# Two attention-convolution layers on one core: bands in four transfers, shorter table slots, x turned from lanes of seven rows, fold one column later

## The chip, the cores and the metric

The kernel runs on one core of a Trainium2 chip, in float32. The metric is the device time of one execution in microseconds (us), the median of several runs. A profile is one further execution, recorded instruction by instruction and DMA packet by DMA packet.

## What is computed

```python
x = x + layer0(group_norm(x))      # x: 8 x 56 x 56 x 384
x = x + layer1(group_norm(x))

def layer0(x):                     # 12 heads of 32 channels, window of 3 x 3
    v = x @ Wv.T                   # every pixel: a value of 384 channels
    a = x @ Wa.T                   # every pixel: 12 heads x 9 x 9 logits
    attn = softmax(a * 32 ** -0.5, axis=-1)
    out = attn @ patches_3x3(v)    # 9 outputs per pixel, from its 9 neighbours
    y = sum of the 9 outputs, each added at the pixel that it belongs to
    return y @ Wo.T

def layer1(x):                     # 6 heads of 64 channels, window of 3 x 3
    a = softmax(x @ W_attn + b)    # every pixel: 6 heads x 9 weights
    v = x @ W_v + b_v
    y = sum over the 9 neighbours of a * v
    return y @ W_proj + b_proj
```

In layer 0, attention of 9 x 9 followed by the addition comes to one linear map from a 5 x 5 neighbourhood of `v` to each pixel, with weights of its own for each pixel and head.

## The kernel before, in words

**Pairs and columns.** The eight images are taken two at a time: four pairs, in each of which a column is 2 x 56 = 112 rows (`R`). Layer 0 goes through the 4 x 56 columns in one loop (line 1007), a step for each column and `LAG` = 3 steps behind it. All seven columns of eight fill 128 partitions: the eighth column's rows are shared out among the 16 spare partitions of the other seven (`OVER`, `share_out`). Its own step has no attention.

**A step.** `attend` (line 685) projects the column to logits in three parts (`bank<-wa_t`), and to values (`bank<-wv_t`). VectorE subtracts the maximum, ScalarE takes the exponential. One step later `normalise` (line 758) sums on VectorE (`d`, `den`) and multiplies on GpSimd (`at<-at,den`). Two steps later `presum` (line 771) adds on GpSimd what the three columns give to one column's weights (`pre`, 9 x 5 x 12 a row); two of its five slices are copied by ScalarE. Three steps later `fold` (line 806) adds over neighbouring rows: ScalarE writes scaled slices to a weight slot of `wts`, TensorE moves rows by a product with `shift` (`pw<-pre,shift`), VectorE adds. SyncE then writes the slot to a table in HBM (`ztab<-wts`). There are four slots in `wts` (`NWT`), so a new column's slices wait until an older slot has been written.

**Bands.** The output is made by patches of 7 x 7 pixels. For a strip of seven columns (`px`) and one image, the table `ztab0` is read back as a matrix `z` (line 383, `bands`): a partition for each of 11 x 11 source pixels of a patch, and for each of eight patches, seven output rows of 12 heads x 7 columns. The table's lines are skewed by one row for each image row, so that one access pattern picks the right weights. A source pixel touches only five output rows, in places that shift with its row; the other entries are zeros of the table. The kernel before reads all seven rows for all 128 partitions in one transfer (`GROUPS0`), and for this a table slot has 11 rows (`EP0`): three of zeros, five of weights, three of zeros. Layer 1 has a table of its own kind, read as two transfers of 45 partitions (`GROUPS1`). `vp<-vtab` reads the values in the same form. `pc<-z,vp` multiplies both, `po<-yT,wo_t` is the last projection.

**Turning x.** [...] x comes with pixels on rows. For pair 0 TensorE turns it. For pairs 1 to 3 this is done while the pair before is worked on, from column 3 to column 45: a block of four columns each three steps. `stats_load` (line 483) brings a block in four transfers, one for each 96 channels: 28 partitions each, on a partition four rows ("lanes") by four columns by 96 channels. VectorE transposes blocks of 32 x 32 (line 524), and gets 128 places for 112 rows, 16 of them empty; `keep_block` (line 550) writes the 112 to HBM (`xT<-xt`) in 12 pieces a partition. ScalarE sums x and its square for the norm.

**What sets the order.** TensorE and GpSimd run in program order, and after line 1002 ScalarE and VectorE too. Each engine's list follows from the loop: `between(0)` to `between(3)` put the work of older columns behind the parts of the projection. Strips are read by `fetch_v` and `fetch_z` at fixed distances behind the loop (line 1062), counted from `LAG`; contractions and output projections are jobs with due steps after that (`plan`, line 874). SyncE issues nearly all DMAs, in its own program order. After its last column layer 0 runs `LAG` steps without attention; then layer 1 starts, while jobs of layer 0's last strips still run.

Of the kernel before, what the change touches and what calls it, by code (L numbers as in the profile page):

```python
# [8 lines left out]
F32 = mybir.dt.float32  # L9
# [6 lines left out]
def two_outlook_layers(  # L16
# [34 lines left out]
    B, H, W, C = x.shape  # L51
    P = 128
    NCH = C // P
    IMG = 2
    R = IMG * H
    MARGIN = 2
# [6 lines left out]
    XB = 4  # L63
# [6 lines left out]
    HEADS0, HEADS1 = 12, 6  # L70
    D0, D1 = C // HEADS0, C // HEADS1
    K, K2 = 3, 9
    E0 = 2 * K - 1
# [4 lines left out]
    PH = K * HEADS0  # L78
# [5 lines left out]
    PY1, NPY1, SX1, SY1 = 8, 7, PX + 2, 10  # L84
    ROW1 = HEADS1 * PX

    GROUPS0 = (((0, P), (0, 7)),)
    GROUPS1 = (((0, 45), (0, 5)), ((45, 90), (3, 8)))

    EP0, FIRST0 = 11, 3
    EP1, FIRST1 = 11, 4
    SLOT0, SLOT1 = EP0 * ROW0, EP1 * ROW1
    LINE0, LINE1 = SX0 * SLOT0 + ROW0, SX1 * SLOT1 + ROW1
# [4 lines left out]
    QC = NCH * Q  # L101
    NR = 4
    LANES = R // NR

    def by_quadrant(ap, r0, col, n, b):
        first = r0 * W * C + col * C + b * QC
        return bass.AP(ap.tensor, ap.offset + first, [[W * C, R], [C, n], [1, QC]])
# [94 lines left out]
        outside(0, 0, R + b * PART)  # L202
        outside(NTILE - 1, 2, R + b * PART + PART - 1)

    NZERO = (EP0 - E0) * ROW0
    zeros = const.tile([R, NZERO], F32, name="zeros")
    gpsimd.memset(zeros, 0.0)

    def fill(table, first, dims, width):

        src = zeros[: dims[0][1], :width]
        if len(dims) > 1:
            src = src.unsqueeze(1).to_broadcast([dims[0][1], dims[1][1], width])
        tc.keep_in_program_order(
            nc.sync.dma_start(bass.AP(table.tensor, table.offset + first, [*dims, [1, width]]), src)
        )
# [22 lines left out]
    def clear_first():  # L239

        clear_v(vtab0, SX0, 2)
        fill(ztab0[0], MARGIN * LINE0 + FIRST0 * ROW0, [[LINE0, R], [SLOT0, 2]], E0 * ROW0)
        clear_weights(ztab0[0], LINE0, 366, SX0, SLOT0, ROW0, FIRST0, E0, EP0)

    def clears():

        yield 3, lambda: clear_weights(
            ztab0[1], LINE0, 366, SX0, SLOT0, ROW0, FIRST0, E0, EP0
        )
        yield (NPAIR - 1) * W + 4, lambda: clear_v(vtab1, SX1, 1)  # L250
        for n, t in enumerate(ztab1):
            yield (NPAIR - 1) * W + 10 + 8 * n, lambda t=t: clear_weights(
                t, LINE1, 350, SX1, SLOT1, ROW1, FIRST1, K, EP1
            )
# [214 lines left out]
    def layer0(late, pools):  # L469
# [6 lines left out]
        stats, st1s, params, xins, attns, pres, xrs, xts = {}, {}, {}, {}, {}, {}, {}, {}  # L476

        def block_tile(pair, blk):
            t = io.tile([P, XB * NCH * P], F32, tag="xt", name=f"xt_{pair}_{blk}")
            n = P if pair else R  # L480
            return t[:, : XB * NCH * n].rearrange("p (m i r) -> p m i r", m=XB, i=NCH)

        def stats_load(pair, blk, queue, xr):
            xrs[pair, blk] = xr
            if not pair:
                queue.dma_start(xr, xf[:R, blk * XB : (blk + 1) * XB, :])
                return
            for b in range(NQ):
                queue.dma_start(
                    xr[b * Q : b * Q + LANES].rearrange("p s m c -> p (s m c)"),  # L490
                    by_quadrant(x, pair * R, blk * XB, XB, b),
                )

        xr_bufs = [io.tile([P, XB * C], F32, tag=f"xr{n}", name=f"xr_{n}", bufs=1) for n in range(2)]
        for t in xr_bufs:
            vector.memset(t[P - Q :], 0.0)

        def xr_tile(pair, blk):
            t = xr_bufs[blk % 2]
            if not pair:  # L500
                return t[:R].rearrange("r (m c) -> r m c", m=XB)
            return t.rearrange("p (s m c) -> p s m c", s=NR, m=XB)

        NWT = 4
        wts = fixed.tile([P, NWT, E0 * HEADS0 * PX], F32, name="wts0")
# [2 lines left out]
        def stats_chunk(pair, blk, i):  # L508

            if blk == 0 and i == 0:  # L510
                if pair:
                    stats[pair] = Sums(f"0_{pair}", NBLK)
                else:
                    stats[pair] = stat.tile([P, IMG, NCH, NBLK, 6], F32, tag="st0", name=f"st0_{pair}", bufs=1)
            if i == 0 and pair:
                xts[pair, blk] = block_tile(pair, blk)
            xr, xt = xrs[pair, blk], xts[pair, blk]
            if pair == 0:
                pt = bank(P, 0, XB * R).rearrange("p (m r) -> p m r", m=XB)
                for j in range(XB):  # L520
                    transpose(pt[:, j, :], xr[:, j, i::NCH], ident[:R, :R])
                scalar.copy(xt[:, :, i, :], pt)
            else:
                vector.transpose(
                    xt[:, :, i, :].rearrange("p m (k s) -> p s m k", s=NR), xr[:, :, :, i::NCH]
                )
            yield
            if pair == 0:
                for b in range(IMG):
                    vector.bn_stats(stats[pair][:, b, i, blk, :], xt[:, :, i, b * H : (b + 1) * H])  # L530
            if i == NCH - 1:
                del xrs[pair, blk]
                if pair:
                    keep_block(pair, blk)
                    if blk == 0:
                        stats[pair].start(lambda b, i: xt[:, :, i, b * H : (b + 1) * H])
                    summed.append((stats[pair], blk, xt.rearrange("p m i r -> p i m r")))
            yield
# [11 lines left out]
        def keep_block(pair, blk):  # L550

            tc.keep_in_program_order(
                nc.sync.dma_start(
                    xTs[pair][:, blk * XB : (blk + 1) * XB].rearrange("p m i r -> p (m i) r"),
                    xts.pop((pair, blk)).rearrange("p m i r -> p (m i) r")[:, :, :R],
                )
            )

# [199 lines left out]
        def normalise(pair, c):  # L758

            nm, at = f"0_{pair}_{c}", attns[pair, c]  # L760
            d4 = work.tile([P, K, 4, PH], F32, tag="d4", name=f"d4_{nm}", bufs=1)
            vector.tensor_add(d4, at[:, :, 0:4], at[:, :, 4:8])
            vector.tensor_add(d4[:, :, 0:2], d4[:, :, 0:2], d4[:, :, 2:4])
            vector.tensor_add(d4[:, :, 0], d4[:, :, 0], d4[:, :, 1])
            den = work.tile([P, K, PH], F32, tag="den", name=f"den_{nm}", bufs=1)
            vector.tensor_add(den, d4[:, :, 0], at[:, :, 8])
            vector.reciprocal(den, den)
            vector.tensor_mul(den, den, inside[:, c % SB].unsqueeze(2).to_broadcast([P, K, PH]))
            gpsimd.tensor_tensor(at, at, den.unsqueeze(2).to_broadcast([P, K, K2, PH]), ALU.mult)

        def presum(pair, c):


            pre = work.tile([R, K2, E0, HEADS0], F32, tag="pre", name=f"pre_{pair}_{c}")

            def of(t, f, n):

                a = attns.get((pair, c + t))
                if a is None:
                    return None  # L780
                a = a[:R].rearrange("r pi (qi qj) (pj h) -> r (pi qi) qj pj h", qj=K, pj=K)
                return a[:, :, 1 - t, f - 1 - t : f - 1 - t + n, :]

            def put(f, n, *terms):
                dst, terms = pre[:, :, f : f + n, :], [t for t in terms if t is not None]
                if len(terms) == 1:
                    gpsimd.tensor_copy(dst, terms[0])
                else:
                    gpsimd.tensor_tensor(dst, terms[0], terms[1], ALU.add)

            put(1, 2, of(0, 1, 2), of(-1, 1, 2))
            yield
            put(3, 1, of(0, 3, 1), of(1, 3, 1))
            put(2, 1, pre[:, :, 2:3, :], of(1, 2, 1)) if c + 1 < W else None
            pres[pair, c] = pre
            yield
            for f, t in ((0, -1), (4, 1)):
                term = of(t, f, 1)
                if term is None:
                    gpsimd.memset(pre[:, :, f : f + 1, :], 0.0)  # L800
                else:
                    scalar.copy(pre[:, :, f : f + 1, :], term)
            attns.pop((pair, c - 1), None)
            yield

# [158 lines left out]
        def upkeep(step):  # L964

            pair, c = divmod(step, W)
            if pair == 0:
                if c == 1:
                    gpsimd.memset(wts, 0.0)
                if c == 3:  # L970
                    by = z_flat[0][:, : NCH * C].rearrange("p (i n) -> p i n", i=NCH)
                    sync.dma_start(by, wo0.rearrange("(i p) n -> p i n", p=P))
                if 5 <= c < 5 + NCH:
                    by = z_flat[0][:, : NCH * C].rearrange("p (i n) -> p i n", i=NCH)
                    sort_columns(wo_t, by, c - 5, vector.tensor_copy)
# [27 lines left out]
        xins.update({blk: homes[blk] for blk in range(4)})  # L1003
        normed(0, WHOLE, both=True)
        normed(1, SHARED, both=True)
        LAG = 3
        for step in range(NPAIR * W + LAG):
            folding = fold(*divmod(step - LAG, W)) if step >= LAG else iter(())
            turning = turned(step)
# [401 lines left out]
```

## Time and profile before

| | us |
|---|---|
| median of three timed runs | 3240.69 (3239.91 to 3242.24) |
| profiled execution, its own time | 3246.89 |
| its span, first to last instruction | 3245.2 |
| PE busy / DVE / ACT / POOL | 3043.9 / 2015.7 / 1386.3 / 1551.5 |

PE is TensorE, DVE VectorE, ACT ScalarE, POOL GpSimd, SP SyncE. Layer 0 takes the first two thirds of the span; its pairs begin at 68, 582, 1108 and 1629 us. The page's row of DMA load has 16 engines; "share" is the part of their time that packets took. A wait in an answer on waits reads: who waited for whom, us in total, times, longest.

The trace also holds every packet. Those of SyncE's queue can be told apart by their size:

| transfer | packet | direction | partitions of SBUF | packets, 582 to 1108 us | mean ns | median ns |
|---|---|---|---|---|---|---|
| `z<-ztab` | 2352 B | in | 128 | 16384 | 107.0 | 95 |
| `vp<-vtab` | 1536 B | in | 128 | 16325 | 72.3 | 65 |
| `xin<-xT` | 5376 B | in | 128 | 1792 | 279.9 | 206 |
| `xr<-in_x` | 384 B | in | 28 | 25088 | 33.3 | 22 |
| `xT<-xt` | 448 B | out | 128 | 21504 | 28.6 | 26 |
| `ztab<-wts` | 1008 B | out | 112 | 9408 | 53.2 | 46 |

Elsewhere: `ztab<-zeros` (2016 B, out of 112 partitions) 96.0 and 82 between 68 and 320 us; in layer 1 between 2250 and 3200 us `z<-ztab` (840 B into 45 partitions) 69.6 and 65, of which the fastest twentieth takes 40; `vp<-vtab` (1536 B into 90 partitions) 104.6 and 104; `out<-ot` (384 B, out of 28 partitions) 23.7 and 22.

### The profile page before, as it was taken

How to read it: one execution, taken by the hardware profiler on the slowest of the kernel's cores; microseconds unless marked ns; L12 is line 12 of the kernel's file. 1: busy time of each engine (PE TensorE's matmuls, PEld its weight loads, DVE VectorE, ACT ScalarE, POOL GpSimd, SP SyncE). 2: the span in 40 equal slices, each digit the busy share in tenths (PEclk: the TensorE clock that was granted, in tenths of full speed). 3: DMA queues.
4: the chain of work that ended last, by engine and by line, in shares of the span. 5: the costliest groups of instructions: out<-in, count | busy, mean ns of one | idle time of the engine just before them, and what ended most of it. 6: DMA issues, size and time to landing. Idle time of an engine off the chain costs nothing. (4 is left out here: it accounts for less than half of the span.)

```text
span 3245.2 us, 72428 instructions
## 1 busy us (share of the span) xinstructions
PE 3043.9 (94%) x27136; PEld 2041.3 (63%) x27136; DVE 2015.7 (62%) x4519; ACT 1386.3 (43%) x3584; POOL 1551.5 (48%) x2319
## 2 busy tenths in 40 slices
PE   6789999998999999998999999979999999999998
PEld 5556666666666766666666677645655656655655
DVE  5767766767776677776666666614545554545454
ACT  4345554555555455555454454433221312222221
POOL 2654554554455555555555555544343334343431
PEclk8899999999999999999999999989999999999998
DMA  9799997899999899999788897788889889989997
GB/s 287 210 280 293 302 290 255 274 294 285 281 274 308 255 276 297 288 300 287 252 274 274 286 303 247 254 309 219 227 229 234 240 231 238 239 233 233 240 232 160
DMA packets 745409, 850.83 MB, mean 262 GB/s; under 512 B 406286, under 2 KB 632210, under 8 KB 736738
## 3 DMA queue, kind: packets, MB, share of 16 engines
q1 hardware_dynamic: 647890, 711.32, 75.4%
q0 software_dynamic: 63824, 116.90, 11.6%
q10 hardware_dynamic: 33344, 17.98, 2.1%
q8 instruction: 214, 3.51, 0.5%
q14 instruction: 137, 1.12, 0.1%
HBM read 514.86 MB, written 322.17 MB: 258 GB/s over the span
## 5 line engine op out<-in xcount | busy, mean ns | idle before, releaser
L128 PE MATMUL bank<-wa_t,xn 128*128 128x288 f32 x3528 | 978.9, 415 | 4.0 <-ACT xn L143 4.0
L128 PE MATMUL po<-yT,wo_t 128*128 128x448 f32 (+1 forms) x2304 | 826.0, 501 | 43.1 <-ACT yT L143 23.5
L143 POOL TENSOR_TENSOR at<-at,den 128x972 f32<-128x972 f32 x196 | 442.4, 2257 | 801.2 <-DVE den L143 441.3
L128 PEld LDWEIGHTS bank<-wa_t,xn 128*128 128x128 f32 x3528 | 658.2, 193 | 216.6 <-issue 19.0
L128 PEld LDWEIGHTS po<-yT,wo_t 128*128 128x128 f32 x2304 | 439.6, 192 | 361.3 <-issue 199.6
L143 ACT COPY yT<-pc 128x294 f32<-128x294 f32 (+2 forms) x512 | 192.4, 401 | 727.4 <-PE pc L128 727.0
L1185 POOL DMA_DIRECT2D at<-lgt x392 | 204.8, 526 | 595.0 <-DVE lgt L143 585.0
L128 PE MATMUL bank<-wc_t,xn 128*128 128x438 f32 x1176 | 477.1, 542 | 1.3 <-DMA wc_t<-in_wv 1.3
L143 DVE TENSOR_REDUCE mx<-bank 128x36 f32<-128x324 f32 x588 | 279.4, 475 | 314.7 <-PE bank L128 312.9
L128 PEld LDWEIGHTS pc<-z,vp 121*32 121x32 f32 (+1 forms) x17664 | 340.6, 121 | 149.8 <-issue 99.9
L128 PE MATMUL pc<-z,vp 121*32 121x49 f32 (+1 forms) x17664 | 377.4, 219 | 44.9 <-issue 19.1
L143 ACT ACTIVATE at<-at 128x972 f32<-128x972 f32 (+1 forms) x228 | 215.2, 944 | 475.2 <-DVE at L143 474.2
L128 PE MATMUL bank<-wv_t,xn 128*128 128x384 f32 x1176 | 416.5, 491 | 0.0
L128 PEld LDWEIGHTS bank<-wc_t,xn 128*128 128x128 f32 x1176 | 215.0, 190 | 176.2 <-issue 163.1
L143 POOL TENSOR_TENSOR pre<-at,at 112x108 f32<-112x108 f32 (+1 forms) x440 | 239.4, 544 | 166.7 <-DMA at<-last 80.7
L128 PEld LDWEIGHTS bank<-wv_t,xn 128*128 128x128 f32 x1176 | 222.8, 191 | 132.7 <-issue 10.2
L143 DVE TENSOR_TENSOR at<-bank,mx 128x324 f32<-128x324 f32 x588 | 291.3, 495 | 20.3
L143 POOL DMA_DIRECT2D vtab<-v x476 | 289.4, 612 | 16.2 <-DMA vtab<-zeros 6.8
L143 ACT ACTIVATE unused<-x1t,shift 128x672 f32<-128x672 f32 (+1 forms) x256 | 200.7, 784 | 178.1 <-DVE x1t L143 152.9
L143 ACT ACTIVATE wts<-pre,inside 112x48 f32<-112x48 f32 (+4 forms) x672 | 179.7, 355 | 207.6 <-DMA ztab<-wts 189.4
L143 DVE TENSOR_TENSOR lgt<-bank,ba_t 128x54 f32<-128x54 f32 x196 | 42.1, 215 | 308.2 <-PE bank L128 303.5
L372 POOL DMA_DIRECT2D vtab<-v x392 | 211.6, 544 | 14.2 <-issue 7.0
(120 smaller groups left out, 2847.3 us busy)
## 6 DMA issues: line engine op xcount, KB each, us to landing
z<-ztab SPq DMA_DIRECT2D x64, 2352.0 KB
vp<-vtab SPq DMA_DIRECT2D x64, 1536.0 KB
vp<-vtab SPq DMA_DIRECT2D x64, 945.0 KB
xres<-xT SPq DMA_DIRECT2D x32, 1176.0 KB
ztab<-wts SPq DMA_DIRECT2D x336, 110.2 KB
vtab<-v POOLq DMA_DIRECT2D x108, 336.0 KB, 6.8
xin<-xT SPq DMA_DIRECT2D x52, 672.0 KB
z<-ztab SPq DMA_DIRECT2D x128, 258.4 KB
```

The lines of the kernel that those rows point to most:

```text
L128: tc.keep_in_program_order(nc.tensor.matmul(*args, **kwargs))
L143: return lambda *args, **kwargs: tc.keep_in_program_order(op(*args, **kwargs))
L372: queue.dma_start(bass.AP(table.tensor, table.offset + first, [*([line * step, count] for step, count in rows_of or ((1, rows),)), *([[(R ...
L1185: nc.gpsimd.dma_start(at_of(g_of)[row : row + n, m_of].rearrange("r k h -> r (k h)"), lg[lo : lo + n])
```

## The change

- `GROUPS0`: a band is read in four transfers of 32 partitions, with the three or six rows that can differ from zero there. The rest of `z` is set to zero once, in six pieces on GpSimd in columns 8 to 13.
- `EP0`: a table slot has 8 rows instead of 11; lines and zero fills get shorter.
- x is loaded so that a partition holds seven rows of two columns: eight transfers of 16 partitions a block instead of four of 28, as many packets of 384 B. Two transposes of 7 x 32 take the place of one of 16 x 32, and give 112 places without gaps, so that `xT<-xt` is one piece of 5376 B a partition.
- `LAG` goes from 3 to 4; the fold and all reads and jobs behind it move by a step. `pre` has three buffers instead of two, and `den` is a part of `d4` that is free by then.
- The two copies of `presum` go from ScalarE to GpSimd.

```diff
@@ -84,13 +84,13 @@
     PY1, NPY1, SX1, SY1 = 8, 7, PX + 2, 10
     ROW1 = HEADS1 * PX
 
-    GROUPS0 = (((0, P), (0, 7)),)
+    GROUPS0 = (((0, 32), (0, 3)), ((32, 64), (0, 6)), ((64, 96), (1, 7)), ((96, P), (4, 7)))
     GROUPS1 = (((0, 45), (0, 5)), ((45, 90), (3, 8)))
 
 
 
 
-    EP0, FIRST0 = 11, 3
+    EP0, FIRST0 = 8, 3
     EP1, FIRST1 = 11, 4
     SLOT0, SLOT1 = EP0 * ROW0, EP1 * ROW1
     LINE0, LINE1 = SX0 * SLOT0 + ROW0, SX1 * SLOT1 + ROW1
@@ -101,6 +101,7 @@
     QC = NCH * Q
     NR = 4
     LANES = R // NR
+    NS = 2 * R // Q
 
     def by_quadrant(ap, r0, col, n, b):
         first = r0 * W * C + col * C + b * QC
@@ -202,7 +203,7 @@
         outside(0, 0, R + b * PART)
         outside(NTILE - 1, 2, R + b * PART + PART - 1)
 
-    NZERO = (EP0 - E0) * ROW0
+    NZERO = C
     zeros = const.tile([R, NZERO], F32, name="zeros")
     gpsimd.memset(zeros, 0.0)
 
@@ -239,13 +240,15 @@
     def clear_first():
 
         clear_v(vtab0, SX0, 2)
-        fill(ztab0[0], MARGIN * LINE0 + FIRST0 * ROW0, [[LINE0, R], [SLOT0, 2]], E0 * ROW0)
-        clear_weights(ztab0[0], LINE0, 366, SX0, SLOT0, ROW0, FIRST0, E0, EP0)
+        for n in range(2):
+            first = MARGIN * LINE0 + FIRST0 * ROW0 + n * SLOT0
+            fill(ztab0[0], first, [[LINE0, R], [E0 * ROW0 // 2, 2]], E0 * ROW0 // 2)
+        clear_weights(ztab0[0], LINE0, 267, SX0, SLOT0, ROW0, FIRST0, E0, EP0)
 
     def clears():
 
         yield 3, lambda: clear_weights(
-            ztab0[1], LINE0, 366, SX0, SLOT0, ROW0, FIRST0, E0, EP0
+            ztab0[1], LINE0, 267, SX0, SLOT0, ROW0, FIRST0, E0, EP0
         )
         yield (NPAIR - 1) * W + 4, lambda: clear_v(vtab1, SX1, 1)
         for n, t in enumerate(ztab1):
@@ -476,9 +479,8 @@
         stats, st1s, params, xins, attns, pres, xrs, xts = {}, {}, {}, {}, {}, {}, {}, {}
 
         def block_tile(pair, blk):
-            t = io.tile([P, XB * NCH * P], F32, tag="xt", name=f"xt_{pair}_{blk}")
-            n = P if pair else R
-            return t[:, : XB * NCH * n].rearrange("p (m i r) -> p m i r", m=XB, i=NCH)
+            t = io.tile([P, XB * NCH * R], F32, tag="xt", name=f"xt_{pair}_{blk}")
+            return t.rearrange("p (m i r) -> p m i r", m=XB, i=NCH)
 
         def stats_load(pair, blk, queue, xr):
             xrs[pair, blk] = xr
@@ -486,20 +488,20 @@
                 queue.dma_start(xr, xf[:R, blk * XB : (blk + 1) * XB, :])
                 return
             for b in range(NQ):
-                queue.dma_start(
-                    xr[b * Q : b * Q + LANES].rearrange("p s m c -> p (s m c)"),
-                    by_quadrant(x, pair * R, blk * XB, XB, b),
-                )
+                for n in range(2):
+                    lo = b * Q + n * Q // 2
+                    queue.dma_start(
+                        xr[lo : lo + Q // 2].rearrange("p s m c -> p (s m c)"),
+                        by_quadrant(x, pair * R, blk * XB + n * XB // 2, XB // 2, b),
+                    )
 
         xr_bufs = [io.tile([P, XB * C], F32, tag=f"xr{n}", name=f"xr_{n}", bufs=1) for n in range(2)]
-        for t in xr_bufs:
-            vector.memset(t[P - Q :], 0.0)
 
         def xr_tile(pair, blk):
             t = xr_bufs[blk % 2]
             if not pair:
                 return t[:R].rearrange("r (m c) -> r m c", m=XB)
-            return t.rearrange("p (s m c) -> p s m c", s=NR, m=XB)
+            return t[:, : XB // 2 * NS * QC].rearrange("p (s m c) -> p s m c", s=NS, c=QC)
 
         NWT = 4
         wts = fixed.tile([P, NWT, E0 * HEADS0 * PX], F32, name="wts0")
@@ -521,9 +523,11 @@
                     transpose(pt[:, j, :], xr[:, j, i::NCH], ident[:R, :R])
                 scalar.copy(xt[:, :, i, :], pt)
             else:
-                vector.transpose(
-                    xt[:, :, i, :].rearrange("p m (k s) -> p s m k", s=NR), xr[:, :, :, i::NCH]
-                )
+                for n in range(XB // 2):
+                    vector.transpose(
+                        xt[:, n :: XB // 2, i, :].rearrange("p m (k s) -> p s m k", s=NS),
+                        xr[:, :, n, i::NCH],
+                    )
             yield
             if pair == 0:
                 for b in range(IMG):
@@ -551,8 +555,8 @@
 
             tc.keep_in_program_order(
                 nc.sync.dma_start(
-                    xTs[pair][:, blk * XB : (blk + 1) * XB].rearrange("p m i r -> p (m i) r"),
-                    xts.pop((pair, blk)).rearrange("p m i r -> p (m i) r")[:, :, :R],
+                    xTs[pair][:, blk * XB : (blk + 1) * XB].rearrange("p m i r -> p (m i r)"),
+                    xts.pop((pair, blk)).rearrange("p m i r -> p (m i r)"),
                 )
             )
 
@@ -762,7 +766,7 @@
             vector.tensor_add(d4, at[:, :, 0:4], at[:, :, 4:8])
             vector.tensor_add(d4[:, :, 0:2], d4[:, :, 0:2], d4[:, :, 2:4])
             vector.tensor_add(d4[:, :, 0], d4[:, :, 0], d4[:, :, 1])
-            den = work.tile([P, K, PH], F32, tag="den", name=f"den_{nm}", bufs=1)
+            den = d4[:, :, 1]
             vector.tensor_add(den, d4[:, :, 0], at[:, :, 8])
             vector.reciprocal(den, den)
             vector.tensor_mul(den, den, inside[:, c % SB].unsqueeze(2).to_broadcast([P, K, PH]))
@@ -771,7 +775,7 @@
         def presum(pair, c):
 
 
-            pre = work.tile([R, K2, E0, HEADS0], F32, tag="pre", name=f"pre_{pair}_{c}")
+            pre = work.tile([R, K2, E0, HEADS0], F32, tag="pre", name=f"pre_{pair}_{c}", bufs=3)
 
             def of(t, f, n):
 
@@ -799,7 +803,7 @@
                 if term is None:
                     gpsimd.memset(pre[:, :, f : f + 1, :], 0.0)
                 else:
-                    scalar.copy(pre[:, :, f : f + 1, :], term)
+                    gpsimd.tensor_copy(pre[:, :, f : f + 1, :], term)
             attns.pop((pair, c - 1), None)
             yield
 
@@ -970,6 +974,9 @@
                 if c == 3:
                     by = z_flat[0][:, : NCH * C].rearrange("p (i n) -> p i n", i=NCH)
                     sync.dma_start(by, wo0.rearrange("(i p) n -> p i n", p=P))
+                if 8 <= c < 14:
+                    b, n = divmod(c - 8, 3)
+                    gpsimd.memset(zs[b][:, 3 * n : min(NPY0, 3 * n + 3)], 0.0)
                 if 5 <= c < 5 + NCH:
                     by = z_flat[0][:, : NCH * C].rearrange("p (i n) -> p i n", i=NCH)
                     sort_columns(wo_t, by, c - 5, vector.tensor_copy)
@@ -1003,7 +1010,7 @@
         xins.update({blk: homes[blk] for blk in range(4)})
         normed(0, WHOLE, both=True)
         normed(1, SHARED, both=True)
-        LAG = 3
+        LAG = 4
         for step in range(NPAIR * W + LAG):
             folding = fold(*divmod(step - LAG, W)) if step >= LAG else iter(())
             turning = turned(step)
```

## The prediction

> **What bounds the kernel now.** The profiled execution took 3246.89 us (span 3245.2, 1.7 around it), 6.2 above the median of the three timed runs, 3240.69. I read the stretches first, cut where layer 0 changes its load: pair 1 with the turning of pair 2's x (600 to 1010), its end without turning (1010 to 1108), the same for pair 2, then pair 3, which turns nothing (1629 to 2029). Columns are the stretch, its length, the busy time of PE, PEld, DVE, ACT and POOL, the granted clock, DMA share and GB/s.
>
> ```profile
> 600.00:1010.00 410.00, 382.15 (x3802) 268.07 (x3801) 293.60 (x688) 227.40 (x573) 214.44 (x284) 0.98 0.95 288
> 1010.00:1108.00 98.00, 92.39 (x715) 63.84 (x714) 63.71 (x168) 52.87 (x133) 52.96 (x71) 0.98 0.77 248
> 1126.00:1530.00 404.00, 379.66 (x3799) 266.52 (x3798) 293.93 (x689) 227.71 (x573) 214.17 (x282) 0.98 0.98 292
> 1629.00:2029.00 400.00, 390.65 (x4057) 277.54 (x4056) 266.31 (x674) 194.72 (x499) 224.27 (x297) 1.00 0.84 277
> ```
>
> With turning, the DMA engines are at 0.95 to 0.98 and PE has gaps; without it DMA falls to 0.84, PE fills and more matmuls go through (4057 in 400 us against 3802 in 410). The first matmul of column 46 comes 443.0, 438.1 and 409.1 us after that of column 0 in pairs 1, 2 and 3 by the rows of `wv_t`. So three times some 30 us hang on DMA load, in the turning stretches. Layer 1 has PE at 99 to 100% in nearly every 100 us; little changes there.
>
> Next, who waits, in pair 1 (582 to 1108), in three answers: ACT's waits, PE's, and SyncE's own.
>
> ```profile
> ACT at L143 <- DVE at L143: 94.7, 40, 7.6
> ACT wts L143 <- DMA ztab<-wts: 59.6, 17, 9.2
> ```
>
> ```profile
> PE po L128 <- ACT yT L143: 7.0, 2, 3.8
> PE pw L128 <- issue: 6.8, 5, 2.8
> PE pw L128 <- POOL pre L143: 5.4, 3, 1.8
> PE pw L128 <- ACT pre L143: 4.7, 1, 4.7
> ```
>
> ACT stands 59.6 us until a weight slot has been written out; in pair 3 that wait is 8.5. [...] ACT's later work (`yT`, `pre`) queues behind the wait. DMA is what has to be costed.
>
> **Costs on the DMA engines, per pair.** The table ahead gives packet times; a sum over 16 engines is count x mean / 16. Pair 1 keeps them busy 0.923 x 526 = 486 us.
>
> (a) *Bands.* Now 16 x 1024 = 16384 packets of 2352 B: 16384 x 107 / 16000 = 109.6 us. After: 8192 of 1008 B and 8192 of 2016 B, bytes down from 2352 to 1512 KB a band. Packets of these sizes exist: median 46 ns (`ztab<-wts`) and 82 ns (`ztab<-zeros`), both out of SBUF. If bands ran like that, with the 12% that 2352 B has over its own 95: 8192 x (52 + 92) / 16000 = 74, a gain of 36. But every load into fewer than 128 partitions is slow in this trace: layer 1's bands (45 partitions, 840 B) take 69.6 at a fastest of 40, 1.74 times; its `vp` (90 partitions) takes 104.6 where layer 0's equal packets into 128 take 72.3. By 1.74: 8192 x (80 + 143) / 16000 = 114, a loss of 5. [...] The nearest row is 45 wide, the change 32, so I go between: **+12** (-36 to +21).
>
> (b) *x loads.* Per block four transfers of 28 partitions become eight of 16, still 1792 packets of 384 B. Now 25088 x 33.3 / 16000 = 52.2 us. [...] From the trace: 1536 and 2352 B into 128 partitions differ by 30 ns for 816 B, 27 B/ns[...]. By the row they replace alone, nothing changes. [...] **+30** (0 to +41).
>
> (c) *Turned x written out.* 21504 packets of 448 B, 28.6 ns, 38.4 us, become 1792 of 5376 B; `xin<-xT`, the same size inward, takes 206 at the median and 280 in the mean: 23 to 31. **-11** (-15 to -7).
>
> Sum +31 a pair: 517 for 486. The turning stretch holds three quarters of the bands and all of the rest, +28. Its engines already run near full; the heaviest 100 us slices show 0.99. Pair 1: (0.95 x 410 + 28) / 0.99 = 422, +12. Pair 2: (0.98 x 404 + 28) / 0.99 = 428, +24. Pair 0 between 200 and 488 (0.96 of 288, some 19 of the 28): 299, +11. **+47.** Pair 3 gets its bands' +12 at a share of 0.84: nothing.
>
> **The rest.**
> - *LAG 4 at the start.* Up to 320 us PE waits for `pw` 7.7 + 4.0 and 9.4 + 5.5 + 5.1 us, the fold being right behind the presum. A column between takes part of it, but DVE and POOL set the pace there (DVE 103 of 132 us from 68 to 200). With the first table's zero fill (1232 packets of 2016 B at 96 ns to 1008 B at 54, 3.2 us, at 92 to 118 us): **-8** (-15 to 0).
> - *LAG 4 elsewhere.* In the turning stretches the `pw` waits give way to the next DMA wait. In the three stretches without turning (DMA 0.77) **-3** (-12 to 0).
> - *LAG 4 at the end.* One more step without attention. The last `pw` groups start 3 to 5 us apart (2113.90, 2117.18, 2121.92, 2126.16): **+4** (0 to +8).
> - *Copies to POOL.* 440 x 282 ns leave ACT (26 a pair), 440 x 276 (POOL's four like copies) join POOL, 30 a pair, at the column's end. Queued behind are the next column's `pre` and `at` multiply. POOL waits 105.7 us a pair for DVE's `den`, which covers them; uncovered, +30 a pair. What ACT gains is lost in its DMA wait: 0.
> - *Transposes.* 126 of 512 elements at 1132 ns become 252 of 224. The `ot` transposes (512: 1107, 384: 887) give 1.72 ns an element over 227, so 612 each: +92 ns x 42, 4 us a pair on DVE, which waits 74 us a pair for PE; 4 if uncovered. `den` inside `d` makes the next column's first add wait for POOL's multiply; at 2096.96 that had ended 1.5 us before. 0 to 4 in all.
> - *z memsets.* Four of 1764 and two of 1176 elements at 0.86 ns (4704 take 4038): 8 us on POOL in columns 8 to 13 of pair 0, POOL half idle: 0.
> - *SyncE.* It issues in order. `xr` issues take 1.46 us (median 0.9) in pair 1, `z` 0.42. 56 more of the first (50 at 0.9) and 48 of the second (20) lift SyncE from 357 to some 427 of 526 us; behind them wait the table writes that ACT waits for. 0 taken; up to +30 a pair.
>
> Sum 47 - 8 - 3 + 4 = +40: 3246.9 + 40 = 3287 profiled, 3240.7 + 40 = **3281** in the timed runs, 1.2% slower.
>
> **Rivals.**
> 1. *Narrow transfers run at full pace* (faster). Bands -36, x loads 0, write-out -11: DMA in the turning stretch falls by 38 to some 350 of 410 and PE bounds it as in pair 3. 34 + 29 and, for pair 0, 21 us of head room, 70% kept since DVE still turns (294 us against 266): -59, with -7 from LAG and a third of the 8 us by which columns 46 to 54 are slower than pair 3's, three times (-8): -74, 3167. Speaking for it: 36% fewer band bytes. It decides when the band packets come under 177 ns for the two sizes together, the x packets costing what I forecast (52), or under 235 if those stay at 33; forecast: 80 to 88 and 148 to 160.
> 2. *Bands as layer 1's, x loads unchanged* (slightly faster): +5 + 0 - 11, -5 in each stretch, -15, and -7: 3219. For it: the x loads are narrow already.
> 3. *SyncE becomes the bound* (much slower): its 427 us grow by the slower issue[...] (`ztab<-wts` takes 1.0 us in pair 1, 0.5 in pair 3). +20 a pair on top: 3340. Against it: 100 us of slack.
>
> **Chances.** Forecast mechanism 0.63, rival 1 0.16, rival 2 0.12, rival 3 0.09. A measurement here tells 0.2%, 6.5 us. The forecast's own range, 3230 to 3330, holds a little of "same"; rival 2 also. Slower 0.67, same 0.06, faster 0.27. Range 3175 to 3340; the slower cases alone 3247 to 3345.
>
> **What would show it.** Right: in the packet records 384 B over 45 ns, 1008 and 2016 B bands at 75 and 145 or more; DMA share near 1 in the turning stretches; ACT's `wts` wait at 60 us a pair or above; column 46 after 450 us in pairs 1 and 2, 409 in pair 3. Wrong: band packets near 50 and 90, DMA share under 0.9, `wts` waits like pair 3's, column 46 after 420. The LAG step: `pw` waits before 320 us at a third, one more `pw` gap at the end. [...]

## The result, and the profile after

| | before | after |
|---|---|---|
| median of four timed runs, us | 3241.03 (3239.91 to 3242.24) | 3282.32 (3278.08 to 3291.92) |
| profiled execution, us | 3246.89 | 3278.08 |
| its span, us | 3245.2 | 3276.3 |

The changed kernel is 1.3% slower: ratio 1.0131, 95% interval 1.0109 to 1.0154. That is +41 us by the medians, and +31 between the two profiles: the profile of before lies 6 above its median, that of after 4 below. All differences inside the span are read from the profiles, so they have to add up to 31.

The same stretches as before (after's first columns come some 6 us earlier in pair 1 and 15 later in pair 3). Columns: stretch, length, busy time of PE, PEld, DVE, ACT, POOL, granted clock, DMA share, GB/s.

```profile
594.00:1005.00 411.00, 377.22 (x3699) 265.45 (x3698) 288.91 (x727) 209.93 (x486) 233.11 (x366) 0.98 0.93 257
1011.00:1111.00 100.00, 93.67 (x894) 65.44 (x895) 63.39 (x169) 48.30 (x112) 55.75 (x88) 0.97 0.77 221
1129.00:1538.00 409.00, 373.31 (x3589) 261.97 (x3587) 285.14 (x719) 207.95 (x482) 231.40 (x362) 0.97 0.93 256
1644.00:2044.00 400.00, 388.15 (x3852) 276.39 (x3851) 261.07 (x662) 175.45 (x405) 241.26 (x379) 0.99 0.90 250
```

Two things to see. In the turning stretches the DMA share did not rise to 1: it fell, from 0.95 and 0.98 to 0.93, and yet PE is busy for less of the time (373 of 409 us in pair 2, where it was busy for 380 of 404). The counts of matmuls say less, since `pc` products come in groups of 96 or 192. In pair 3, which turns nothing, the share rose from 0.84 to 0.90. ScalarE waits for weight slots more than before, 84.7 us in pair 1 for 59.6:

```profile
ACT wts L144 <- DMA ztab<-wts: 84.7, 17, 9.7
```

PE no longer waits for `pre`, but for landings and for what hangs on them (pair 1):

```profile
PE po L129 <- ACT yT L144: 10.4, 3, 4.3
PE pc L129 <- DMA z<-ztab: 8.0, 1, 8.0
```

SyncE's queue waits for landings, too. First before (582 to 1108), then after (582 to 1110):

```profile
SPq L143 <- DMA ztab<-wts: 12.2, 6, 5.7
SPq L143 <- DMA z<-ztab: 3.4, 2, 3.2
SPq L143 <- DMA vp<-vtab: 2.4, 2, 1.4
```

```profile
SPq L144 <- DMA z<-ztab: 44.3, 34, 2.8
SPq L144 <- DMA vp<-vtab: 25.7, 8, 4.3
SPq L144 <- DMA ztab<-wts: 23.2, 17, 5.5
```

Most of SyncE's DMAs depend on nothing that these transfers bring. In the traces its DMAs (1901 before, 2262 after) share eight semaphores, and each waits until the DMA that had its own last, nearly always eight places before, has landed. So at most eight are in flight.

Packets of SyncE's queue, by size, 582 to 1108 us; the last three rows come from the experiments. The 1008 B of bands and of `ztab<-wts` are in one row; taking the latter at 53.2 ns, the bands' own come to some 78 in after and 83 in "bands alone".

| kernel | 384 B in: mean, median ns | 1008 B | band packets of 2016 B |
|---|---|---|---|
| before | 33.3, 22 | 53.2, 46 (table writes) | none; 2352 B: 107.0, 95 |
| after | 29.3, 22 | 64.6, 46 | 160.0, 164 |
| bands alone (32 neighbours) | 32.5, 22 | 67.1, 51 | 158.9, 162 |
| two bands (64 neighbours) | 32.6, 22 | 57.2, 46 (table writes) | 157.8, 164 |
| bands stepped (every fourth) | 32.3, 22 | 53.1, 46 | 97.4, 82 |

Where the 31 us lie, by the first matmul of each pair's column 0, with the parts in runs of their own (length of each in us by the profile):

| kernel | start | pair 0 | pair 1 | pair 2 | pair 3 | layer 1 | span |
|---|---|---|---|---|---|---|---|
| before | 68.4 | 513.5 | 526.3 | 521.3 | 521.3 | 1094.4 | 3245.2 |
| after | 62.6 | 513.5 | 535.0 | 533.1 | 538.7 | 1093.4 | 3276.3 |
| e1, after with one band | 61.9 | 515.2 | 522.0 | 522.6 | 517.2 | 1092.0 | 3230.8 |
| e2, bands alone | 67.9 | 516.7 | 525.4 | 525.9 | 533.4 | 1091.5 | 3260.7 |
| e3, x alone | 63.2 | 525.6 | 522.7 | 533.4 | 520.7 | 1095.2 | 3260.8 |
| e4, after with LAG 3 | 64.8 | 523.6 | 534.3 | 535.0 | 538.6 | 1093.5 | 3289.8 |
| e5, x split | 67.7 | 543.5 | 547.4 | 548.6 | 520.2 | 1096.7 | 3324.0 |
| e10, copies on POOL | 67.9 | 524.5 | 525.3 | 518.9 | 529.1 | 1092.4 | 3258.1 |
| e12, bands stepped | 68.1 | 496.0 | 498.6 | 504.0 | 519.6 | 1092.4 | 3178.6 |

After against before: -6 at the start, 0, +9, +12, +17, -1. Each row is one execution, and lies up to 9 us off the median of its kernel (e1 9 below it, e12 6 above), so small differences between rows say little.

### The profile page after: what moved, and what is told of

Read it like the earlier page. It is cut to its first block, busy times and chain, and to the rows that moved or that the text cites. A ratio compares the mean times of both kernels' runs of the same rounds, so it can differ in the third digit from the quotient of the medians.

```text
span 3276.3 us, 72832 instructions
## 1 busy us (share of the span) xinstructions
PE 3051.1 (93%) x27136; PEld 2048.5 (63%) x27136; DVE 1998.9 (61%) x4643; ACT 1300.3 (40%) x3144; POOL 1666.2 (51%) x2765
## 5 line engine op out<-in xcount | busy, mean ns | idle before, releaser
L144 POOL TENSOR_TENSOR at<-at,d 128x972 f32<-128x972 f32 x196 | 441.7, 2253 | 649.7 <-DVE d L144 398.7
## 6 DMA issues: line engine op xcount, KB each, us to landing
z<-ztab SPq DMA_DIRECT2D x128, 504.0 KB
```

What stands on the lines that cost most here:

```text
L144: return lambda *args, **kwargs: tc.keep_in_program_order(op(*args, **kwargs))
```

## Experiments

Ratios are to runs of the kernel before on the same chip (medians 3239.2 for e1 to e4, 3236.8 for e5 to e8, 3237.9 for e9 to e11, 3239.7 for e12). Brackets are 95% intervals of the ratio. Three theories stood at first: A, the narrow bands cost the time; B, the later fold; C, the 16-partition x loads.

**e1: the changed kernel with the bands of before.**

```diff
-    GROUPS0 = (((0, 32), (0, 3)), ((32, 64), (0, 6)), ((64, 96), (1, 7)), ((96, P), (4, 7)))
+    GROUPS0 = (((0, P), (0, 7)),)
...
-    EP0, FIRST0 = 8, 3
+    EP0, FIRST0 = 11, 3
...
```

> The changed kernel with the bands as before: one transfer of 128 partitions and seven rows, table slots of 11 rows. Theory A (the narrow band transfers cost the time; the other parts cost nothing or gain): below the kernel before, 3195 to 3230 us, band packets of 2352 B at 107 ns again, ACT's wait for the table writes under 60 us in pair 1. Theory B (the fold a column later costs it, by the order of work that it shifts): 3275 to 3290. Theory C (the x loads of 16 partitions cost it): 3270 to 3290.

Measured 3242.2, ratio 1.0010 [0.9998, 1.0021]. So the bands make all of the difference on top of the other parts, but those gain nothing, against A's 3195 to 3230.

**e2: the kernel before with the bands of the change** (groups, slots, zero fills, `z` memsets; the diff of e1 the other way round).

> The kernel before with the bands alone changed: four transfers, slots of 8 rows, z zeroed once. Theory A: slower than the changed kernel or like it, 3280 to 3320 us, packets of 2016 B at 160 ns. Theories B and C: as before, 3235 to 3250.

Measured 3265.4, 1.0080 [1.0063, 1.0097]: +26, under A's span and over that of B and C. B and C alone fall here, as they do in e1.

**e3: the kernel before with the x loads, transposes and write-out of the change.**

```diff
-                queue.dma_start(
-                    xr[b * Q : b * Q + LANES].rearrange("p s m c -> p (s m c)"),
-                    by_quadrant(x, pair * R, blk * XB, XB, b),
-                )
+                for n in range(2):
+                    lo = b * Q + n * Q // 2
...
```

> The kernel before with only x turned from lanes of seven rows. Theory A: as before or a little faster, 3220 to 3242 us (384 B packets at 29 ns, the write-out in 5376 B packets, some 10 us of DMA time less per pair). Theory C: slower, 3265 to 3285. Theory B: as before.

Measured 3263.4, 1.0078 [1.0060, 1.0095]: +24. So A alone falls as well: two parts cost about as much each. But its packets of 384 B take 30 ns, not 52, and the DMA share of pair 1 falls to 0.89. C has the part right and the reason wrong.

**e4: the changed kernel with `LAG` 3** (and `pre` and `den` as before).

> The changed kernel with the fold at its old distance of three columns, two pre buffers and den in a tile of its own. Theory A: 3275 to 3305 us, like the changed kernel or slower, as TensorE waits for pre again. Theory B: 3235 to 3255. Theory C: 3275 to 3290.

Measured 3286.9, 1.0148 [1.0133, 1.0163], 5 slower than the changed kernel by the medians, with intervals that overlap: the later fold is a small gain at most, and no loss. In the table it lies in pair 0 (523.6 to 513.5).

A fourth theory, D, was made from e3's trace: small loads fill SyncE's window of eight.

**e5: the kernel before with each x load cut in two**, nothing else changed in layout.

```diff
+                for n in range(2):
+                    lo, r0 = b * Q + n * LANES // 2, pair * R + n * R // 2
+                    src = by_quadrant(x, r0, blk * XB, XB, b)
                     queue.dma_start(
-                        ...
+                        xr[lo : lo + LANES // 2].rearrange("p s m c -> p (s m c)"),
+                        bass.AP(src.tensor, src.offset, [[W * C, R // 2], [C, XB], [1, QC]]),
```

> The kernel before with each of the four loads of a block of the next pair's x cut into two of 14 partitions: eight loads of 224 packets of 384 B, as many as in the changed kernel, but with the layout, transposes, packet sizes, bytes and write-out of before. Theory C (the 16-partition loads, or what hangs on their layout, is what the x part costs): no change, 3236 to 3246. Theory D (SyncE keeps at most eight DMAs in flight, since each waits for the one eight places before it; more and smaller DMAs fill that window with fewer bytes): +15 to +30, 3254 to 3270, with the DMA share of the turning stretches lower than before, not higher, and with SyncE waiting for landings of z and table writes for tens of us in pair 1 where before it hardly waits.

Measured 3328.8, 1.0289 [1.0257, 1.0322]: +92, three times D's upper end, and all in the pairs that turn (+30, +21, +27). So eight loads for four are enough to lose the time, whatever the lanes. That e3 loses less, by its shorter issues and its cheaper write-out (27 us a pair for 38), is argued, not shown. The rows of these loads (issue on SyncE, ns: minimum, median, maximum) for before, x split and x alone tell how many bytes SyncE's issue brings in:

```profile
L143 SPq DMA_DIRECT2D xr<-in_x x56: 804/896/5145, 585.9 to 967.0; - x56
```

```profile
L143 SPq DMA_DIRECT2D xr<-in_x x112: 800/802/2305, 615.1 to 1019.8; - x112
```

```profile
L144 SPq DMA_DIRECT2D xr<-in_x x112: 578/613/3307, 593.0 to 973.8; - x112
```

An issue of half the bytes takes as long (800 ns for 14 partitions, 804 for 28) or somewhat less (578 for 16). A load of 28 partitions is 172 KB: 214 GB/s at the shortest issue. Half of it is 107 GB/s, and 86 KB in 613 ns 140, less than the 288 GB/s that the engines move in before's stretch. The DMA share while SyncE issues them shows it. Over the first 40 columns of pairs 1 and 2, from the trace (load is the packets' time over 16 engines, idle what is left; packets overlap in these records, so that some shares pass 1):

| kernel | length | load | idle | share while x loads are issued | while SyncE waits for a landing |
|---|---|---|---|---|---|
| before | 426, 421 | 408, 412 | 18, 10 | 0.94, 0.96 | 0.94, 0.97 |
| e5, x split | 447, 450 | 405, 409 | 43, 41 | 0.77, 0.78 | 0.97, 0.96 |
| e3, x alone | 423, 433 | 387, 390 | 36, 44 | 0.83, 0.79 | 1.00, 0.93 |
| after | 430, 432 | 400, 401 | 30, 31 | 0.80, 0.81 | 1.01, 1.00 |
| e2, bands alone | 425, 429 | 418, 420 | 7, 8 | 0.94, 0.94 | 0.99, 1.01 |
| e12, bands stepped | 404, 409 | 386, 384 | 18, 25 | 0.93, 0.92 | 0.98, 0.97 |

The last column speaks against D: while SyncE waits for its window the engines are full. They run dry while it issues small loads (0.77 to 0.83 for before's 0.94 and 0.96). In e5 this is as clear as it gets: the load is before's to 3 us, and the engines idle 25 to 31 us longer.

**e6: the kernel before with the x loads issued by GpSimd**, to take them out of SyncE's window.

```diff
-                stats_load(pair + 1, blk + 1, sync, xr_tile(pair + 1, blk + 1))
+                stats_load(pair + 1, blk + 1, gpsimd, xr_tile(pair + 1, blk + 1))
```

> The kernel before with the loads of the next pairs' x (168 DMAs) issued by GpSimd instead of SyncE, everything else as it was. Theory D: SyncE's window of eight then holds only bands, table writes and the like, so ACT's wait for the weight slots shrinks from 59.6 us in pair 1 to 20 to 45 and the time falls by 5 to 40 us, 3200 to 3235, unless GpSimd's issue costs it as much as it gains. DMA load alone as the bound (my prediction): the load is the same, no change, 3234 to 3246.

Measured 3259.4, 1.0066 [1.0042, 1.0090]: slower, a miss for D. SyncE is relieved, and the engines' load rises instead: from 582 to 1108 us GpSimd's queue holds them for 96.0 us (before: 47.4), SyncE's for 395.2 (434.7), together 9 more. The x loads' own packets are not the reason. They come as 3840 and 4224 B and take 45 us for 52; but SyncE's other packets take 13 us longer (2352 B 111.3 ns for 107.0, 1536 B 76.1 for 72.3). So packets of one size took more or less time with what else was under way. With load at 417 of 423 us in the first 40 columns of pair 1 nothing is gained.

**e7: the changed kernel with one band of five rows into all 128 partitions.** It leaves out the outer two of a band's seven rows, and with them weights that belong there, so it serves as a timing only.

```diff
-    GROUPS0 = (((0, 32), (0, 3)), ((32, 64), (0, 6)), ((64, 96), (1, 7)), ((96, P), (4, 7)))
+    GROUPS0 = (((0, P), (1, 6)),)
```

> The changed kernel with one transfer per band into all 128 partitions, rows 1 to 5 only (16 per pair of 1680 B packets x 1024 x ...): rows 0 and 6 of the band are left out, so the folded weights of those rows are stale; the table slots stay short. Bytes are near those of the four narrow transfers (1720 KB... 128 x 8 x 1680 B a band against 1548), but the count of DMAs is before's. Theory A[...]: well under the after kernel, 3215 to 3242. Theory D (count): the same, since the count falls; against the kernel with one band of seven rows (3242) it tells what bytes are worth: 3225 to 3242 if DMA load still bounds the turning stretches, 3240 to 3246 if it doesn't.

Measured 3192.6, 0.9859 [0.9836, 0.9881]. Each packet has 1680 B, 82.6 ns: 16384 x 82.6 / 16000 = 85 us a pair for the 122 of the four narrow transfers, with 11% more bytes. It is some 90 us faster than the changed kernel, and 50 faster than e1, which differs by packets of 2352 B and longer slots. So bytes and packet time count even where the engines' share is 0.88 to 0.91: D's "the same, since the count falls" is no explanation of the 50. First e1, then e7:

```profile
594.00:1005.00 411.00, 387.21 (x3824) 273.22 (x3823) 292.45 (x738) 212.94 (x495) 239.63 (x375) 0.97 0.91 294
```

```profile
572.00:983.00 411.00, 390.90 (x3940) 275.33 (x3938) 302.20 (x769) 222.04 (x518) 246.44 (x383) 0.98 0.88 275
```

**e8: e1 with the x loads issued by GpSimd.**

> The changed kernel with the bands of before (one transfer, long slots) and with the loads of the next pairs' x issued by GpSimd: the parts x lanes, fold a column later and copies on GpSimd, without the eight x loads a block in SyncE's window. With SyncE's queue it took 3242. Theory D: the x loads' price of some 20 us goes away, 3205 to 3230. DMA load or GpSimd as the bound (its columns get 336 issues more beside the copies): 3240 to 3265.

Measured 3236.5, 1.0000 [0.9989, 1.0010]; e1 had 1.0010. The gain that D expected isn't there. The trace shows why: in the first 40 columns of pairs 1 and 2 the engines idle only 15 and 17 us, for 37 and 38 in e1, but their load is 410 and 406 us for 382 and 385. Again SyncE's packets take longer beside GpSimd's (2352 B 117.1 ns for 106.5, 1536 B 83.2 for 73.6). So the idle time does come with small loads on SyncE, and this way of removing it costs as much as it saves.

**e9: the kernel before with two transfers of 64 partitions per band.** It asks what makes the band packets slow, the number of transfers (32 a pair here, 64 in the change) or the places that they go to, here 64 neighbours. The expectation has the number first, then the places. The rest of `z` is set to zero as in the change.

```diff
-    GROUPS0 = (((0, P), (0, 7)),)
+    GROUPS0 = (((0, 64), (0, 6)), ((64, P), (1, 7)))
...
```

> The kernel before with two transfers per band, rows 0 to 5 into partitions 0 to 63 and rows 1 to 6 into 64 to 127 (packets of 2016 B, 14% fewer bytes), slots as before, and the z memsets that this needs. If narrowness costs by the count of DMAs alone (32 a pair for 16; four narrow ones were 64): 2016 B packets near 95 to 105 ns, load -5 to -12 us a pair, 3220 to 3245. [...] packets of 2016 B stay at 150 to 165 ns as in the four narrow transfers, load +40 to +55 us a pair, 3320 to 3400.

Measured 3401.0, 1.0500 [1.0476, 1.0523], a microsecond past the upper end for the places. Packets of 2016 B take 164 ns at the median, as much as with 32 neighbours (164 in the changed kernel, 162 in e2). So half the transfers don't make them shorter; e12 below has the other half of the comparison. Pair 1 in e9, stretch and ScalarE's wait:

```profile
637.00:1047.00 410.00, 362.26 (x3331) 253.02 (x3331) 273.64 (x643) 213.76 (x539) 196.61 (x261) 0.95 0.98 256
```

```profile
ACT wts L143 <- DMA ztab<-wts: 94.3, 19, 14.2
```

There are 14% fewer band bytes than before, and fewer GB/s at a full share: 256 at 0.98, where before had 288 at 0.95. A busy engine isn't one that moves much.

**e10 and e11: the copies.** e10 is the kernel before with only the copies on GpSimd, e11 the changed kernel without them.

```diff
-                    scalar.copy(pre[:, :, f : f + 1, :], term)
+                    gpsimd.tensor_copy(pre[:, :, f : f + 1, :], term)
```

> The kernel before with the 440 copies into pre moved from ScalarE to GpSimd, nothing else. My prediction: 0, 3233 to 3243. From the runs so far, where the parts fold a column later and copies together took 21 us off the kernel with the x lanes, and fold a column later alone 5: 3220 to 3232.

> The changed kernel with the 440 copies left on ScalarE. My prediction: as the changed kernel, 3275 to 3288. If the copies on GpSimd are what took 15 us off: 3290 to 3305, with ScalarE's work of some 124 us more and its waits for weight slots less by no more than a part of that.

e10: 3256.4, 1.0048 [1.0030, 1.0066], +18: slower, against both expectations. e11: 3285.2, 1.0147 [1.0124, 1.0170], 3 over the changed kernel, no difference that can be told. Alone the copies cost, and the waits of PE in pair 0 (68 to 582 in before, 68 to 592 in e10) say where:

```profile
PE pw L128 <- POOL pre L143: 13.1, 5, 7.7
```

```profile
PE pw L128 <- POOL pre L143: 42.1, 17, 7.2
```

All `pw` waits of that pair come to 30.6 us before (13.1, 12.4 for "issue", 5.1 for ScalarE's copy) and 42.9 in e10; pair 0 is 11 longer. In pair 3 the POOL row grows from 3.5 to 11.1, the pair by 8. `pre` is ready later on GpSimd, and a fold one step behind it has to wait. With `LAG` 4 it doesn't: e4, which has the copies but not the later fold, shows 35.3 us of such waits on `pre` in pair 0, the changed kernel none. The two edits belong together.

**e12: the bands of the change, spread over the partitions.** The 32 slots of a transfer go to every fourth partition instead of 32 neighbours. `vp` must have its rows in the same places, so it comes in four transfers. The expectation begins with the case that the places set the packets' time.

```diff
-                z[s0:s1, :, m0 * row : m1 * row],
+                (z[s0 // 32 :: 4] if row == ROW0 else z[s0:s1])[:, :, m0 * row : m1 * row],
...
-            rows_to_patches(sync, vps[pair, px, b], vtab0, px, b * H, PY0, NPY0, SX0)
+            for g in range(4):
+                rows_to_patches(sync, vps[pair, px, b][g::4], vtab0, px, b * H, PY0, NPY0, SX0, 32 * g)
...
-                                vp[: SX0 * SY0, py, h * D0 : (h + 1) * D0],
+                                vp[:, py, h * D0 : (h + 1) * D0],
```

> The kernel before with the part bands of the change, but the 32 slots of each transfer go to every fourth partition (0, 4, 8 ..., then 1, 5, 9 ...) instead of 32 neighbouring ones, and the v patches are loaded in four transfers to the same partitions (48 DMAs a pair more), the products then summing over all 128. With 32 neighbours it took 3265. [...] 1008 B at 46 to 55 ns and 2016 B at 85 to 100, so 67 to 79 us a pair for the bands in place of 122, the load of the turning stretches down by 25 to 40 us, 3160 to 3215, faster than both kernels. If it is the 32 partitions as such, whichever they are: packets as before, 3265 to 3300. If SyncE's issue of 96 more DMAs a pair is what counts: the packets short, and still 3230 to 3275.

Measured 3173.8, 0.9794 [0.9774, 0.9813]: 66 us faster than before, 108 faster than the changed kernel by the medians, with 96 more DMAs a pair than before. The packets of 2016 B take 82 ns at the median, half of the 164. Their sizes, their number and the width of 32 are those of e2, so the difference lies in the places. `vp` in four transfers gains nothing by itself (1536 B: 74.5 ns, for 72.7 in e2). Bands cost 8192 x (53 + 97) / 16000 = 77 us a pair. The stretches and ScalarE's wait in pair 1:

```profile
590.00:990.00 400.00, 383.33 (x3680) 269.11 (x3670) 302.94 (x721) 239.90 (x605) 223.20 (x295) 1.00 0.94 275
1600.00:2000.00 400.00, 389.95 (x3690) 275.16 (x3689) 266.43 (x675) 194.78 (x500) 225.12 (x298) 1.00 0.80 249
```

```profile
ACT wts L143 <- DMA ztab<-wts: 15.5, 9, 3.4
```

The wait for weight slots falls from 59.6 to 15.5. Column 46 comes after 415 and 420 us in pairs 1 and 2, near pair 3's 409, and pair 3 itself stays at its old length (519.6): there PE is busy for 390 of 400 us, and little is left to win by DMA.

## Why the prediction was right in its time, and where its steps failed

- **What bounds it: right in part.** Where the bands' packets get cheaper (e7, e12) the time falls, and where they get dearer (e9) it rises. But load alone does not set the time: pair 1 grew by 9 us at before's load, and in e5 by 21.
- **(a) Bands, +12 a pair: right.** The 78 and 160 ns give 8192 x 238 / 16000 = 122 us for 110. Layer 1's row gave 114; what the forecast put on top, and its upper end of +21, were the author's estimate, for which no trace had a figure. Where the packets land made it: 162 ns against 82 for the same packets (e2, e12). The runs vary the places; why they count, none of them shows. The lengths that the forecast drew from the 12 did not come: in e2 pairs 0 to 2 grow by 7 us together and pair 1 not at all, since the engines' idle time took the load up (18 to 7 us in 40 columns of pair 1).
- **But "pair 3 gets its bands' +12: nothing" failed.** In e2 pair 3 loses most, 12 of the 19 us by which the four pairs grow. A share of 0.84 is an average: the load comes in lumps (in before, stretches of 20 us between 1629 and 2029 us have shares from 0.47 to 1.06), and ScalarE's slot waits there and at the change of layers go from 16.2 us (1629 to 2150) to 30.6. In the changed kernel they are 54.9, and PE waits 12.1 us at the end of layer 0 where before's longest there is 6.5. First before (2103 to 2155), then after (2123 to 2187):

```profile
PE pc L128 <- DMA z<-ztab: 6.5, 1, 6.5
```

```profile
PE pc L129 <- DMA ztab<-wts: 12.1, 1, 12.1
```

- **(b) x loads, +30: wrong.** The forecast of 52 ns failed: 29.3, down from 33.3, so 25088 x 29.3 / 16000 = 46 us, -6 in place of +30. The +30, and its upper end of +41, were the author's estimate, for which no trace had a figure. The reading that goes with it, that every load into fewer than 128 partitions is slow in this trace, had a counterexample in its own table: 384 B into 28 partitions took 22 ns at the median, as much as out of 28. Consecutive transfers are short and go to different partitions; whether that is why was not shown.
- **(c) Write-out, -11: right.** 1792 x 245 / 16000 = 27 for 38 (245 ns is the mean of this size, reads of `xin` included).
- **Sum a pair, 517: wrong by (b).** Pair 1 holds 0.904 x 535 = 484, no more than before's 486. "DMA share near 1" failed with it. With what the packets took the forecast's own sum is +12 - 6 - 11 = -5 a pair, nearly rival 2's -6, from which that rival made 3219: the costs of rival 2 came, and the time of the forecast. The step from DMA load to time is what does not hold.
- **Column 46: short of the forecast.** After 450 us was forecast in pairs 1 and 2, and 409 in pair 3; measured are 444.6, 444.8 and 411.9. Part of that is order: with `LAG` 3 (e4) they are 449.6, 450.2 and 421.9 in pairs of the same length.
- **SyncE, 0 taken: the other error, of opposite sign.** The time that the forecast gave to slower packets of x shows as idle engines instead, 12 to 21 us more in 40 columns, and they idle while SyncE issues loads of 86 KB. e5 shows that the number of loads is enough for this; that the bytes of an issue set it is argued. Rival 3 had the place, not the form: SyncE wasn't full. Its time in pair 1 didn't grow (296 us, where 427 were forecast and before had 357); what it issued was small.
- **LAG: right.** Forecast were -8 up to 320 us, -3 elsewhere and +4 at the end. After against e4 gives -2 before the first column, -10 in pair 0 and -1 in the other pairs, but -5 by the medians. The `pw` waits before 320 us fell from 28.1 us to 5.2, under the forecast third; no added wait shows at the end, so nothing of the +4 is seen.
- **Copies, 0: right for the changed kernel, but for another reason.** Not POOL's waits for `den` cover them, as e10 shows, but the later fold.
- **Transposes, +4 at most:** cheaper than forecast, 588 ns for 612:

```profile
L144 DVE STREAM_TRANSPOSE xt<-xr 128x224 f32<-128x224 f32 x252 | 128.3, 588 | 1.8
```

- **The places.** Forecast were +11, +12 and +24 in pairs 0 to 2 and nothing but LAG in pair 3. Measured are 0 (with LAG's -10 in it), +9, +12 and +17, and -6 at the start, which was not forecast. It comes with the x part (63.2 us in e3), and the trace shows from what. In before the first load of x has to wait for VectorE's memset of the last 32 partitions of `xr` (1.34 us, ends at 2.53); it is issued at 2.56 us, after ScalarE's load of the weights (2.19), and its packets start at 7.7 us, after those of the weights (5.3). The change drops this memset: the load is issued at 0.81, its packets start at 1.8, and the first product on x at 6.5 us instead of 14.7. PE's waits for x before 320 us, first before, then after:

```profile
PE bank L131 <- DMA xr<-in_x: 20.3, 8, 14.7
```

```profile
PE bank L132 <- DMA xr<-in_x: 13.2, 7, 6.6
```

- **Rival 1** put its turn at 177 ns for a 1008 B and a 2016 B packet together, and its time at 3167. With other partitions (e12) they take 151, and the time is 3174.

The total of +40 against +41 is thus in good part luck: 36 us of load a pair that aren't there (+31 forecast, -5 measured) stood for idle engines and for pair 3. By parts, +26 (e2), +24 (e3), -5 (e4) and -3 (e11) make +42. That they add up so well may be chance: the later fold and the copies, -8 here, took 21 off "x alone" (3263 to 3242). Why they are worth more there than with narrow bands stays open. What the issue alone costs was not isolated with larger loads of the same lanes.

## What to carry to other kernels

Before bytes are cut by splitting a load, see which partitions each piece lands on: here four pieces of 32 neighbours cost 122 us a pair (after), the whole 110 (before), and the same four on every fourth partition 77 (e12). A share of busy DMA engines near 1 says neither that bytes are the limit nor that a smaller load will help (e9 moved 256 GB/s at 0.98, before 288 at 0.95); packet times by size do. Splitting loads can leave the engines idle though not a byte is added (43 and 41 us in e5, 18 and 10 before), so count the bytes that each issue brings in.

## What the runs showed of the hardware

- The time of a 2016 B packet into SBUF doubled with the partitions' places: 82 ns at the median for every fourth of 128 (e12), 164 for 32 neighbours in the changed kernel (162 in e2) and for 64 (e9).
- 384 B packets showed nothing of this: 22 ns at the median into 16 neighbouring partitions (after, e3), 14 (e5) and 28 (before).
- The issue of an x load took 804 ns for 28 partitions of 16 pieces (before), 800 for 14 of 16 (e5), and 578 for 16 of 14 (e3; all minima): it is not proportional to the packets, 448, 224 and 224.
- Packets of one queue took longer beside those of another: with the x loads on GpSimd's queue, 2352 B on SyncE's took 111.3 ns for 107.0 (e6, before) and 117.1 for 106.5 (e8, e1), while the x loads' own packets held the engines for 45 us in place of 52 (e6, pair 1).
